# Quantile aggregation over graph neighbours: a dense layer replaced by gathered neighbour lists

## The chip, the cores and the metric

The kernel runs on one NeuronCore of one Trainium2 chip. The metric is the device time of one execution in microseconds (us). The engines are named as in the profile: PE (TensorE, matrix products), PEld (its weight loads), DVE (VectorE), ACT (ScalarE), POOL (GpSimd), SP (SyncE, which here only issues transfers). SBUF is the on-chip memory of 128 partitions, PSUM the accumulators that PE writes.

## The reference

For 16 graphs (batches) of 1024 nodes with 64 channels, cut to what matters:

```python
h = relu(layernorm(x))                      # x: (16, 1024, 64)
neigh = (adj > 0) & ~eye                    # symmetric, each edge with probability about 1/128
nb, rank = count and running number of the neighbours in each row
skip = where(nb > 10, (nb + 1) // 2, 1)
rem = neigh & (skip > 1) & (rank % skip == skip - 1) & mask;  rem |= rem.T
nd = (adj with 1 on the diagonal, without rem) > 0     # kept neighbours and the node itself
s = sort(where(nd, h[neighbour], inf))      # per node and channel, over the neighbours
nv = nd.sum()
agg = sum over (tau, w) of ((0.25, 0.25), (0.5, 0.5), (0.75, 0.25)):
        w * linear interpolation of s at tau * (nv - 1)
y = (relu((h + agg) @ W1 + b1) @ W2 + b2) * mask       # 64 -> 128 -> 64
return x + y
```

In the inputs of this case (counted from the reference's own data) a node has about 7.5 kept neighbours beside itself and at most 22.

## The kernel before

The kernel takes any adjacency and makes no list of neighbours. Work is cut into pairs of batches and into batches.

`prep_pair` (DVE mostly): layer norm of two batches, a transpose, and a bitonic sort of 128 rows (2 batches x 64 channels) of 1024 values with the node number carried along, 55 compare-exchange stages (L181 to L191, `k`, `i`, `swap`, `move`). The sorted values go to DRAM as three bf16 terms (`sd`). A second bitonic sort (L216, L217) brings the nodes' ranks back into node order.

`prep_batch`: each 128 rows of the adjacency (512 KB, tile `at`) are loaded, compared, and scanned along the row to number the neighbours (`rk`, L254); POOL clears the diagonal with an affine select (`ne` L247, `edges` L271); dropped edges are marked (L266 to L270), and the kept adjacency is transposed on PE (L301).

`main`, per batch: 16 groups of four channels x 2 halves of the nodes x 6 order statistics (two for each of three quantiles) = 192 units. Per group, `weights` builds bucket indicators on DVE (`eq` L362, `wt` L360) and three word weights on POOL (`wt` L365). Per group and half, `pack` multiplies them with the kept adjacency (L374, 32 products) and ACT moves the result from PSUM to SBUF (L378, `packed`). Each unit runs through a chain of small products and elementwise steps on 128 x 512 tiles: `choose` (`oh` L390, `hot` L392), `words` (`sel` L397, `wd` L401, `bits` L404), `locate` (`place` L411/L413, `cand` L416, `hit` L418 on DVE, `hitw` L420 on POOL, `val` L422 on DVE) and `add` (`agg` L426). The units are software-pipelined by hand, one stage of four units in each turn of the loop, and each turn also takes one step of a background generator: the preparation of the next batch or pair. Then come the MLP and the residual.

Each engine works through its own queue in order and waits on semaphores. A scheduler in the build puts the instructions of each engine into an order of its own; an instruction without inputs that wait can move far ahead of where it is written.

Of the kernel before, what the change touches and what calls it, by code (L numbers as in the profile page):

```python
# [24 lines left out]
F32 = mybir.dt.float32  # L25
# [4 lines left out]
I32 = mybir.dt.int32  # L30
U8 = mybir.dt.uint8
# [8 lines left out]
NT = N // P  # L40
NG = 16
NB = 32
HALF = 512
NSEL = 6
WEIGHTS = (0.25, 0.5, 0.25)
EPS = 1e-5
FIELDS = ((0, 11), (11, 11), (22, 10))


@with_exitstack  # L50
def quantile_graph_layer(
# [24 lines left out]
    kb = cst.tile([P, cbf.shape[1]], BF16, name="kb")  # L76
    nc.sync.dma_start(out=kb, in_=cbf)
    kf = cst.tile([P, cf32.shape[1]], F32, name="kf")
    nc.sync.dma_start(out=kf, in_=cf32)
# [37 lines left out]
    xs, hT, rankT, sorted_d = {}, {}, {}, {}  # L117
    nd, bucket, word_w, maskc = {}, {}, {}, {}

# [421 lines left out]
```

## Time and profile before

| what | value |
|---|---|
| median of 3 runs | 18762.58 us (18743.5 to 18764.14) |
| the profiled execution: span, first to last instruction | 18769.8 us |
| its own time beside the span | the page gives none; the span is 7.2 us over the median of the runs |
| PE busy | 15007.5 us, 80% of the span, 55296 products |
| DVE busy | 15816.9 us, 84%, 19847 instructions |
| POOL busy | 7256.0 us, 39%, 4293 instructions |
| ACT busy | 3137.9 us, 17% |
| DMA | 98.46 MB, mean 5 GB/s |

How to read the rows that follow: a group row reads "line, engine, operation, output <- inputs, shape of output <- shape of input, count | busy us of the group, mean ns of one instruction | idle time of its engine just before them and what ended most of it". A timeline row reads "start us, duration us, engine, line, operation". Durations of neighbouring DVE instructions overlap a little in the records, so the distance from start to start tells what one costs in a row of many. The issue of a transfer is not counted as busy time of the engine that issues it.

### The profile page before, as it was taken

What the parts mean: (1) busy time and instruction counts of PE and PEld (TensorE: products, weight loads), DVE (VectorE), ACT (ScalarE), POOL (GpSimd) and SP (SyncE); (2) the same over time, 40 slices, a digit from 0 to 9 for tenths busy, and PEclk for the clock granted to TensorE, in tenths of its full rate; (3) what the DMA queues carried; (4) which work ended last, traced back from release to release, by engine and by line L of the source; (5) the groups of instructions that cost most, each with busy time, mean ns of one, the idle gap of its engine ahead of it and who ended that gap; (6) DMA issues with size and microseconds to landing.
All of it is one profiled execution on the core that took longest, in us unless ns stands there. A gap on an engine that the chain in (4) does not pass through costs nothing. (4 is left out here: it accounts for less than half of the span.)

```text
span 18769.8 us, 153006 instructions
## 1 busy us (share of the span) xinstructions
PE 15007.5 (80%) x55296; PEld 5255.5 (28%) x55296; DVE 15816.9 (84%) x19847; ACT 3137.9 (17%) x5402; POOL 7256.0 (39%) x4293
## 2 busy tenths in 40 slices
PE   2887788777888788887788887888878887788888
PEld 0222222222222222222222222222222222223333
DVE  9898878988789887898878988789887898877777
ACT  0111111111111111111111111111111111111111
POOL 1333443334433344333443334433343333443333
PEclk6999999999999999999999999999999999999999
DMA  0000000000000000000000000000000000000000
GB/s 23 4 1 3 10 8 4 1 3 12 8 2 1 3 12 8 2 1 3 12 8 2 1 3 12 8 2 1 3 12 9 1 2 2 12 6 1 2 1 1
DMA packets 183963, 98.46 MB, mean 5 GB/s; under 512 B 163426, under 2 KB 163618, under 8 KB 183202
## 3 DMA queue, kind: packets, MB, share of 16 engines
q1 hardware_dynamic: 183202, 88.68, 1.8%
q8 instruction: 433, 7.09, 0.2%
q14 instruction: 328, 2.69, 0.0%
HBM read 78.14 MB, written 10.49 MB: 5 GB/s over the span
## 5 line engine op out<-in xcount | busy, mean ns | idle before, releaser
L420 POOL TENSOR_TENSOR hitw<-hit,coef 128x512 bf16<-128x512 bf16 x3072 | 5080.3, 1654 | 9836.9 <-DVE hit L418 9596.5
L426 PE MATMUL agg<-val,kf 128*64 128x512 f32 x6144 | 3445.6, 643 | 2079.5 <-DVE val L422 2071.6
L374 PE MATMUL pk<-kept,wt 128*128 128x512 fp8e4 x16384 | 4170.5, 385 | 278.2 <-POOL wt L365 155.5
L397 DVE TENSOR_TENSOR sel<-packed,hot 128x2048 f16<-128x2048 f16 x3072 | 4090.9, 1335 | 123.3 <-ACT hot L392 115.6
L422 DVE TENSOR_TENSOR val<-cand,hitw 128x512 f32<-128x512 f32 x3072 | 2113.5, 688 | 1976.9 <-POOL hitw L420 1884.2
L401 PE MATMUL wd<-sel,kb 128*128 128x512 f16 x9216 | 2650.1, 391 | 744.4 <-DVE sel L397 742.6
L392 ACT CAST hot<-oh 128x512 f16<-128x512 f32 x3072 | 1797.1, 585 | 7573.1 <-PE oh L390 3841.7
L416 PE MATMUL cand<-hot,table 128*128 128x512 f16 x9216 | 2674.7, 396 | 0.0
L404 DVE TENSOR_SCALAR bits<-wd,ki 128x512 int32<-128x512 int32 x3072 | 2278.7, 742 | 124.4 <-PE wd L401 122.2
L378 ACT ACTIVATE packed<-pk 128x512 f16<-128x512 f32 x2048 | 1223.2, 597 | 6859.8 <-PE pk L374 6858.1
L418 DVE TENSOR_TENSOR hit<-place,want 128x512 bf16<-128x512 f32 x3072 | 2099.5, 683 | 319.2 <-PE place L413 308.0
L374 PEld LDWEIGHTS <-wt 128*128 128x128 fp8e5 x16384 | 1593.4, 99 | 2507.5 <-POOL wt L365 380.5
L365 POOL TENSOR_TENSOR wt<-eq,ww 128x1024 fp8e5<-128x1024 bf16 x768 | 1824.9, 2400 | 724.0 <-DVE eq L362 473.2
L426 PEld LDWEIGHTS agg<-val,kf 128*64 128x64 f32 x6144 | 599.5, 137 | 3576.8 <-DVE val L422 3447.8
L401 PEld LDWEIGHTS <-kb 128*128 128x128 bf16 x9216 | 921.1, 100 | 2088.2 <-issue 1155.6
L413 PE MATMUL place<-bits,kb 128*128 128x512 bf16 x3072 | 1253.2, 408 | 97.9 <-DVE bits L404 96.8
L390 PE MATMUL oh<-below,kb 128*128 128x512 f16 x3072 | 1197.6, 390 | 163.8 <-ACT hot L392 137.9
L383 DVE TENSOR_TENSOR below<-packed,want 128x1536 f16<-128x1536 f16 x1024 | 1254.7, 1225 | 3.9 <-ACT want L337 3.4
L416 PEld LDWEIGHTS <-table 128*128 128x128 bf16 x9216 | 869.5, 100 | 1325.0 <-issue 629.9
L411 PE MATMUL place<-sel,kb 128*128 128x512 f16 x3072 | 1215.8, 396 | 14.6 <-DVE hit L418 14.4
L399 PE MATMUL wd<-hot,kb 128*128 128x512 f16 x3072 | 1200.9, 391 | 0.0
L413 PEld LDWEIGHTS <-kb 128*128 128x128 bf16 x3072 | 304.1, 99 | 1512.5 <-issue 1402.5
(97 smaller groups left out, 7443.2 us busy)
## 6 DMA issues: line engine op xcount, KB each, us to landing
at<-in_adj_dram SPq DMA_DIRECT2D x128, 512.0 KB, 3.6
table<-sd SPq DMA_DIRECT2D x768, 8.0 KB, 1.7
sd<-term SPq DMA_DIRECT2D x24, 256.0 KB, 2.0
xt<-in_x_dram SPq DMA_DIRECT2D x16, 256.0 KB, 4.0
out_dram<-res SPq DMA_DIRECT2D x16, 256.0 KB, 2.6
kb<-in_cbf_dram SPq DMA_DIRECT2D x1, 320.0 KB, 2.7
mu<-in_nodemask_dram SPq DMA_DIRECT2D x16, 1.0 KB, 4.7
kf<-in_cf_dram SPq DMA_DIRECT2D x1, 126.0 KB, 2.6
```

The lines of the kernel that those rows point to most:

```text
L365: nc.gpsimd.tensor_tensor(dst(n + 1), eq, wb, OP.mult, saturate=False)
L374: nc.tensor.matmul(pk, wt[:, t, n, :], kept[:, t, half * HALF:(half + 1) * HALF], start=(t == 0), stop=(t == NT - 1),)
L392: nc.scalar.copy(hot, oh)
L397: nc.vector.tensor_tensor(sel, packed, hot[:, None, :].to_broadcast([P, 4, HALF]), OP.mult)
L401: nc.tensor.matmul(wd, fields[n], sel[:, n + 1], start=False, stop=(n == 2))
L404: nc.vector.tensor_scalar(bits, wd.bitcast(I32), shift, 0x40000000, OP.logical_shift_left, OP.bitwise_and)
L413: nc.tensor.matmul(at, prefix, hi, start=False, stop=True)
L416: nc.tensor.matmul(cand, table[g // 4][:, n, g % 4, :], hot, start=(n == 0), stop=(n == 2))
L418: nc.vector.tensor_tensor(hit, at, want[:, half, s], OP.is_equal)
L420: nc.gpsimd.tensor_tensor(hitw, hit, coef[:, half, s], OP.mult)
L422: nc.vector.tensor_tensor(val, cand, hitw, OP.mult)
L426: nc.tensor.matmul(agg[half], pick[:, 60 - 4 * g:124 - 4 * g], val, start=False, stop=(g == NG - 1 and s == NSEL - 1),)
```

## The change

The dense method stays in the file as `dense_layer`, as a loop over pairs of batches with nothing woven beside it, and runs only if a flag is set. In its place `list_layer` computes all 16 batches:

- `load`, `drop`, `keep`: the same kept adjacency, made on PE and ACT: sign of the adjacency, its transpose, running counts as products with a triangular matrix (`rk`), the dropped edges `rem` (DVE), and the kept edges (`kp`, relu on ACT). `code`: a product that packs each row's kept neighbours as 256 words of four bits.
- `order`: nodes are ordered by their number of kept neighbours, so that the first tile of 128 nodes has the longest lists; `perm` is the permutation as a 0/1 matrix. `rem` and `perm` take turns in one buffer (tag `wide`, bufs=1).
- `collect`: the permuted words (PE), then the largest eight of them at a time with `max` and `match_replace` on DVE, which give the lists in order of neighbour number (`idx`).
- `fetch`: one indirect DMA on POOL's queue per list position and tile of 128 nodes: 128 rows of 64 floats from the table of `h` in DRAM into slot `s` of a tile `g`. By tile the lists hold 13, 11, 11, 10, 9, 8, 7, 6 rows (`CAPS`): 75 gathers for a batch. The 32 nodes with the longest lists of eight batches go through 2 x 24 gathers more (`fetch_group`, tile `gg`).
- `sort`: a sorting network over the slots, each compare-exchange a `min` (L881) and a `max` (L882) on DVE with two SBUF inputs over 128 x (128, 384, 256, 256) floats for a pair of batches (L887 where one end is enough); then each sorted slot times its interpolation weight (L892) and a product with the identity that adds it up in PSUM. `let_go` writes a one-element memset to a tile `pause` (L868) after each 0.8 us of such work as estimated in the code; nothing reads `pause`.
- `finish`: 8 gathers for a batch bring the MLP's rows back into node order; mask, residual, store.
- the main loop fetches pair m, sorts pair m - 1, and weaves the preparation of batches 2m + 2 and 2m + 3 between.
- at the end a flag is 1 if any node had more kept neighbours than its list holds; each engine loads it and branches.

The diff, cut to its core:

```diff
+CAP = 24
+TOP = 19
+CAPS = (13, 11, 11, 10, 9, 8, 7, 6)
+CLASSES = (((0,), 13), ((1, 2, 3), 11), ((4, 5), 9), ((6, 7), 7))
+FEW = 32
+GROUP = 8
...
 @with_exitstack
-def quantile_graph_layer(
+def dense_layer(
...
-    drain(prep_pair(0))
-    drain(prep_batch(0))
-    for pr in range(B // 2):
...
+    with tc.For_i(0, B, 2) as first:
+        first_b.append(first)
+        drain(prep_pair(0))
+        for b in range(2):
+            drain(prep_batch(b))
+            main(b, iter(()))
...
+    def load(b):
...
+            at = wk.tile([P, N], F32, name="at", bufs=2)
+            nc.sync.dma_start(out=at, in_=adj[b, t * P:(t + 1) * P, :])
+            sg = wk.tile([P, N], BF16, name="sg")
+            nc.scalar.activation(sg, at, AF.Sign)
+            for n in range(2):
+                tp = psum.tile([P, 4, P], F32, name="tp", tag="mx", bufs=4)
...
+                nc.scalar.activation(
+                    ne[:, 4 * n:4 * n + 4, t * P:(t + 1) * P], tp, AF.Relu, saturate=False
+                )
...
+    def drop(b):
...
+        rem = wk.tile([P, NT, N], BF16, name="rem", tag="wide", bufs=1)
...
+                nc.scalar.activation(dist[:, n * HALF:(n + 1) * HALF], rk, AF.Abs, bias=bias[:, t:t + 1])
+            nc.vector.tensor_scalar(rem[:, t], dist, half[:, t:t + 1], None, OP.is_equal)
...
+    def keep(b):
...
+                kp = psum.tile([P, 4, P], F32, name="kp", tag="mx", bufs=4)
+                nc.tensor.matmul(kp, plus, ne[:, 4 * n:4 * n + 4, ts], start=True, stop=False)
+                nc.tensor.matmul(kp, minus, rem[:, 4 * n:4 * n + 4, ts], start=False, stop=False)
+                for s in range(4):
+                    at = (4 * n + s) * P
+                    nc.tensor.matmul(kp[:, s], rem[:, t, at:at + P], minus, start=False, stop=(s == 3))
+                nc.scalar.activation(kept[:, 4 * n:4 * n + 4], kp, AF.Relu, saturate=False)
...
+                nc.tensor.matmul(
+                    code[:, s], kept[:, s], nibble, start=(s == 0), stop=(s == NT - 1), skip_group_check=True
+                )
+            nc.scalar.copy(pack[:, t, :KEYS], code.rearrange("p s k -> p (s k)"))
...
+        perm = wk.tile([P, NT, N], BF16, name="perm", tag="wide", bufs=1)
+        for t in range(NT):
+            nc.vector.tensor_scalar(perm[:, t], iota, place_f[:, t:t + 1], None, OP.is_equal)
...
+    def collect(b):
...
+            flat = psum.tile([P, KEYS + 1], F32, name="codeP", tag="code", bufs=2)
+            code = flat[:, :KEYS].rearrange("p (s k) -> p s k", k=33)
+            nc.tensor.matmul(flat, ones16[0:1], base, start=True, stop=False)
+            for t in range(NT):
+                nc.tensor.matmul(flat, perm[:, t, k * P:(k + 1) * P], pack[:, t], start=False, stop=(t == NT - 1))
...
+            for at in range(lo, hi, 8):
+                nc.vector.max(keys[:, at:at + 8], left)
+                if at + 8 < hi:
+                    nc.vector.match_replace(rest, keys[:, at:at + 8], left, 0.0)
+                    left = rest
...
+        idx = wk.tile([P, PASSED[-1] + NT], I32, name="idx", bufs=4)
+        nc.vector.tensor_scalar(idx, found, float(N), 0.0, OP.min, OP.max)
...
+    def fetch(m, halves=(0, 1)):
...
+            for k in tiles:
+                for h in halves:
+                    idx, tab = lists[2 * m + h], tables[2 * m + h]
+                    for s in (*range(CAPS[k] - 1), slots - 1):
+                        at = PASSED[-1] + k if s == slots - 1 else PASSED[k] + s
+                        nc.gpsimd.indirect_dma_start(
+                            out=g[:, s, h, k - tiles[0]], out_offset=None, in_=tab,
+                            in_offset=bass.IndirectOffsetOnAxis(ap=idx[:, at:at + 1], axis=0),
+                        )
...
+    def let_go(held):
+        if held < 0.8:
+            return held
+        nc.vector.memset(pause, 0.0)
+        return 0.0
+    def sort(g, slots, top, coef, acc):
...
+        held = 0.0
+        for lo, hi, low, high in NETWORKS[slots]:
+            pa, pb = where[lo], where[hi]
+            if low and high:
+                nc.vector.tensor_tensor(g[:, spare], g[:, pa], g[:, pb], OP.min)
+                nc.vector.tensor_tensor(g[:, pb], g[:, pa], g[:, pb], OP.max)
+                where[lo], spare = spare, pa
+                yield 2 * cost
+            else:
+                to = pa if low else pb
+                nc.vector.tensor_tensor(g[:, to], g[:, pa], g[:, pb], OP.min if low else OP.max)
+                yield cost
+            held = let_go(held + cost * (low + high))
+        for s in range(top):
+            v = g[:, where[s]]
+            nc.vector.tensor_tensor(v, v, coef(s).to_broadcast(shape), OP.mult)
+            nc.tensor.matmul(acc, ident32, v, start=False, stop=(s == top - 1))
+            held = let_go(held + cost)
...
+    def fetch_group(grp):
...
+        for k in range(n):
+            for s in range(CAP):
+                nc.gpsimd.indirect_dma_start(
+                    out=g[:, s, k], out_offset=None, in_=tab,
+                    in_offset=bass.IndirectOffsetOnAxis(ap=idx[:, k, s:s + 1], axis=0),
+                )
...
+    def finish(b):
...
+        for t in range(NT):
+            nc.gpsimd.indirect_dma_start(
+                out=yn[:, t], out_offset=None, in_=ys[b],
+                in_offset=bass.IndirectOffsetOnAxis(ap=place_of[:, b, t:t + 1], axis=0),
+            )
...
+    def prepare(b):
+        yield from both(drop(b), load(b + 1) if b + 1 < B else iter(()), normalize(b))
+        yield from keep(b)
+        yield from order(b)
+        yield from collect(b)
...
+    drain(load(0), prepare(0))
+    fetch(0, (0,))
+    drain(prepare(1))
+    pairs, per = B // 2, GROUP // 2
+    ready, waiting = [], []
+    for m in range(pairs + 1):
+        begun = [finish(b) for b in ready[:2]]
+        ready = ready[2:]
+        for g in begun:
+            next(g)
+        work = []
+        if m < pairs:
+            if m % per == per - 1:
+                fetch_group(m // per)
+                work.append(aggregate_group(m // per))
+            fetch(m, (0, 1) if m else (1,))
+        if m:
+            work.append(aggregate(m - 1))
+            waiting += [2 * m - 2, 2 * m - 1]
+        side = chain(*(prepare(b) for b in (2 * m + 2, 2 * m + 3) if b < B))
+        weave(chain(*work, *begun, (1.0,)), 115.0 if m else 1.0, side, 85.0)
+        grouped = GROUP * ((m + 1) // per)
+        ready += [b for b in waiting if b < grouped]
+        waiting = [b for b in waiting if b >= grouped]
+    drain(*(finish(b) for b in ready))
...
+    keep = ctx.enter_context(tc.tile_pool(name="keep", bufs=1))
+    flag = keep.tile([1, 1], I32, name="flag")
+    list_layer(tc, x, adj, nodemask, W1, b1, W2, b2, cbf, cf32, out, flag)
+    full = tc.nc.values_load(flag[0:1, 0:1], min_val=0, max_val=1)
+    with tc.If(full > 0):
+        dense_layer(tc, x, adj, nodemask, W1, b1, W2, b2, cbf, cf32, ci32, out)
```

The two programs differ in all their rows, so the places that matter are shown from each apart. POOL's queue in the dense method, somewhat into the program: elementwise products for the units and affine selects for the next batch.

```order
L247 AFFINE_SELECT ne<-ne 128x128
L420 TENSOR_TENSOR hitw<-hit,coef 128x512 x5
L271 AFFINE_SELECT edges<-edges 128x128
L420 TENSOR_TENSOR hitw<-hit,coef 128x512 x3
L365 TENSOR_TENSOR wt<-eq,ww 128x8x128 x3
```

POOL's queue in `list_layer` for the last pair and the second group (tiles g_18313 to g_18440 are the four classes of pair 7, `gg` the group, `yn` the rows of `finish`):

```order
L857 DMA g_18313<-htab,idx 128x64 x13
L857 DMA g_18340<-htab,idx 128x64 x32
L857 DMA g_18313<-htab,idx 128x64 x7
L953 DMA gg<-gtab,gat 128x64 x48
L857 DMA g_18313<-htab,idx 128x64 x6
L857 DMA g_18340<-htab,idx 128x64 x32
L857 DMA g_18405<-htab,idx 128x64 x34
L857 DMA g_18440<-htab,idx 128x64 x26
L977 DMA yn<-yd,place_of 128x64 x64
```

POOL no longer computes: its queue is 1424 gathers in a row (the 150 of each pair, 96 for two groups, 128 for `finish`). The first eight of all have no wait on one another; each later one waits for the one eight places ahead to land.

DVE's queue in the dense method, in the middle of a batch: the elementwise steps of the units (`hit`, `val`, `bits`), with stages of the next pair's sort between them.

```order
L404 TENSOR_SCALAR bits<-wd,ki 128x512
L184 TENSOR_TENSOR k_6740<-k_6646 128x256x2
L187 TENSOR_TENSOR move<-i_6647 128x512
L418 TENSOR_TENSOR hit<-place,want 128x512
L189 TENSOR_TENSOR move<-move,swap 128x512
L182 TENSOR_TENSOR k_6875<-k_6740 128x512
L422 TENSOR_TENSOR val<-cand,hitw 128x512
```

DVE's queue in `list_layer` near the end, where the second group's sort (`gg`) and the first exchanges of pair 7's last tile (g_18440) stand, and then, some 120 rows on, the end of the group's sort and the sort of pair 6 (g_16106 is its first tile):

```order
L881 TENSOR_TENSOR gg<-gg 128x128
L882 TENSOR_TENSOR gg<-gg 128x128
L881 TENSOR_TENSOR g_18440<-g_18440 128x256
L881 TENSOR_TENSOR gg<-gg 128x128
L882 TENSOR_TENSOR g_18440<-g_18440 128x256
```

```order
L892 TENSOR_TENSOR gg<-gg,gcoef 128x128
L882 TENSOR_TENSOR gg<-gg 128x128
L892 TENSOR_TENSOR gg<-gg,gcoef 128x128 x2
L882 TENSOR_TENSOR g_16106<-g_16106 128x128
L881 TENSOR_TENSOR g_16106<-g_16106 128x128
```

The scheduler has put the first exchanges of pair 7 ahead of the sort of pair 6, and so behind them in DVE's queue 590 rows are left: the rest of the group, nearly all of pair 6, and all of pair 7. No memset stands between these exchanges.

DVE's queue at the start of `list_layer`, where constants and the first batch's layer norm are made:

```order
L868 MEMSET pause 128x1 x10
L551 CAST kw<-kb 128x545
L868 MEMSET pause 128x1
L589 TENSOR_SCALAR pack<-kf 128x8
L868 MEMSET pause 128x1 x19
L581 CAST mask<-mu 128x128
L868 MEMSET pause 128x1 x10
L561 CAST iota<-iota_i 128x1024
L868 MEMSET pause 128x1 x6
```

The memsets, which wait for nothing, have moved ahead: of 996, 493 stand before the first exchange of all, 229 directly between two instructions of a sort, and none among the last 1738 of the 2672 instructions of the sorts.

More of the change, by code (lines that the diff above doesn't have):

```diff
@@ L73, in quantile_graph_layer @@
     dram = ctx.enter_context(tc.tile_pool(name="dram", bufs=2, space=bass.MemoryType.DRAM))
[L76 to L79, printed above, removed]
+    kb = cst.tile([P, BF_AT], BF16, name="kb")
+    nc.sync.dma_start(out=kb, in_=cbf[:, :BF_AT])
+    kf = cst.tile([P, F32_AT], F32, name="kf")
+    nc.sync.dma_start(out=kf, in_=cf32[:, :F32_AT])
     ki = cst.tile([P, ci32.shape[1]], I32, name="ki")
@@ L419, in locate @@
             hitw = wk.tile([P, HALF], BF16, name="hitw")
-            nc.gpsimd.tensor_tensor(hitw, hit, coef[:, half, s], OP.mult)
+            nc.vector.tensor_tensor(hitw, hit, coef[:, half, s], OP.mult)
             val = wk.tile([P, HALF], F32, name="val")
@@ new lines, in ones_col, with wanted, batcher @@
+def ones_col(pool, nc):
+    t = pool.tile([P, 1], F32, name="ones_c")
+    nc.vector.memset(t, 1.0)
+    return t
+def wanted(n):
+    return -(-3 * (n - 1) // 4) + 1
+def batcher(n):
+    size = 1 << (n - 1).bit_length()
+    pairs, p = [], 1
+    while p < size:
+        k = p
+        while k >= 1:
+            for j in range(k % p, size - k, 2 * k):
+                for i in range(min(k, size - j - k)):
+                    if (i + j) // (2 * p) == (i + j + k) // (2 * p) and i + j + k < n:
+                        pairs.append((i + j, i + j + k))
+            k //= 2
+        p *= 2
+    return pairs
```

454 lines of the change are left out of this document (437 added, 17 removed), and 4 rows, old and new, of the table SHORT.

## The prediction

> **What bounds the kernel now.** I read the page's engine rows first, then its groups, then the waits, then stretches of the timeline.
>
> ```profile
> PE 15007.5 (80%) x55296; PEld 5255.5 (28%) x55296; DVE 15816.9 (84%) x19847; ACT 3137.9 (17%) x5402; POOL 7256.0 (39%) x4293
> L420 POOL TENSOR_TENSOR hitw<-hit,coef 128x512 bf16<-128x512 bf16 x3072 | 5080.3, 1654 | 9836.9 <-DVE hit L418 9596.5
> L374 PE MATMUL pk<-kept,wt 128*128 128x512 fp8e4 x16384 | 4170.5, 385 | 278.2 <-POOL wt L365 155.5
> L397 DVE TENSOR_TENSOR sel<-packed,hot 128x2048 f16<-128x2048 f16 x3072 | 4090.9, 1335 | 123.3 <-ACT hot L392 115.6
> L378 ACT ACTIVATE packed<-pk 128x512 f16<-128x512 f32 x2048 | 1223.2, 597 | 6859.8 <-PE pk L374 6858.1
> ```
>
> DVE is busy for 84% and PE for 80%: no engine is idle enough to matter, and the 3072 units of the dense method (x3072 in the rows) set the time, 18,770 / 3072 = 6.1 us a unit. So the amount of work bounds it, not one wait. The waits confirm it: the longest that holds DVE is the one for `hitw`, a tenth of the span.
>
> ```profile
> DVE val L422 <- POOL hitw L420: 1884.2, 2049, 3.6
> ```
>
> **The change part by part.** All of the units, both bitonic sorts and the bucket weights go, 15,817 us of DVE and 15,008 us of PE. So the new time is built up from nothing, not subtracted. The sum stands against the profiled execution, span 18,769.8 us, 7 us (0.04%) over the median of the runs shown; beside a change of this size that is nothing.
>
> *DVE.* In a row of many, what counts is start to start.
>
> ```profile
> 107.48 0.67 DVE L181 TENSOR_TENSOR swap<-k 128x512 f16<-128x512 f32 x1
> 108.08 0.41 DVE L187 TENSOR_TENSOR move<-i 128x512 f16<-128x512 f16 x1
> ...
> 210.97 1.22 DVE L211 SCALAR_TENSOR_TENSOR kp<-i,iota 128x1024 f32<-128x1024 f16 x1
> 212.10 1.22 DVE L270 SCALAR_TENSOR_TENSOR edges<-d,ne 128x1024 bf16<-128x1024 bf16 x1
> ...
> 20.15 0.14 DVE L257 TENSOR_SCALAR skip<-rk 128x1 int32<-128x1 f16 x1
> 20.21 0.21 DVE L259 TENSOR_SCALAR many<-rk,mk 128x1 f32<-128x1 f16 x1
> ...
> 21.85 0.48 DVE L266 TENSOR_SCALAR d<-rk,first 128x1024 bf16<-128x1024 f16 x1
> 22.25 0.69 DVE L143 TENSOR_SCALAR h<-h 128x1024 f32<-128x1024 f32 x1
> ```
>
> A fp32 step with two inputs costs 0.60 us for 512 elements and 1.13 for 1024: 0.07 us and 1.04 ns an element. So 128, 256 and 384 elements cost 0.20, 0.34 and 0.47 us. A pair's sorts are 97 instructions of 128, 77 of 384 and 92 of 256 elements: 19 + 36 + 31 = 86 us, and 689 for eight pairs. Two groups: 544 of 128, 109 us. The 996 memsets at the 0.06 to 0.07 us of the [P, 1] steps: 65 us, half of it at the start, where DVE waits for loads anyway. A batch's preparation: `rem` and `perm` 16 x 0.40, 13 maxima and 5 replacements of 256 at 0.34 to 0.42, the rest some 60 small ones: 25 to 28 us, some 420 in all. DVE in sum about 1,270 us.
>
> *PE.* The transposes and fp8 products show two speeds, and the granted clock in the stretches says when (columns: stretch, length, then busy us of PE, PEld, DVE, ACT, POOL; clock; DMA share; GB/s):
>
> ```profile
> 331.58 0.61 PE L301 MATMUL et<-kb,edges 128*128 128x128 bf16 x8 [0.86 <-DVE kept L302]
> 336.58 1.01 PE L301 MATMUL et<-kb,edges 128*128 128x128 bf16 x8 [0.72 <-DVE kept L302]
> 9004.21 1.89 PE L374 MATMUL pk<-kept,wt 128*128 128x512 fp8e4 x8
> 9002.76 1.07 PE L426 MATMUL agg<-val,kf 128*64 128x512 f32 x2 [0.93 <-DVE val L422]
> 100.00:200.00 100.00, 0.00 (x0) 0.00 (x0) 100.00 (x218) 0.00 (x0) 0.00 (x0) 0.50 0.00 0
> 9000.00:9400.00 400.00, 316.82 (x1212) 112.51 (x1212) 340.47 (x400) 67.10 (x116) 178.23 (x104) 0.95 0.05 14
> ```
>
> A product of up to 128 columns costs 0.08 us (0.13 at the lower clock), one of 512 0.24, one of fp32 1.07 for two instructions. A batch has 328 of the first kind, 64 wide ones and 72 of 265 columns: 26 + 14 + 10 with small rest, 59 us, 90 at the low clock; a pair's fp32 products 33. PE in sum 1,200 us, 1,700 at worst: beside DVE, not over it.
>
> *A batch's lists as a chain.* `rem` and `perm` share one buffer, so two batches' lists can't overlap much, and from step to step ACT, PE and DVE wait for one another. From ACT's 0.60 us per 128 x 512 eviction: `drop` with the next `load` 32 evictions and 8 signs of 1,024 elements, 27 us; `keep` 16 and 8 shorter ones, 20 with its products; `order` 8; `perm` 3; `collect` 18 + 7. That is 84, with hand-overs 94 us (an estimate). Four batches stand at the start, where nothing else covers them: 4 x 94 and a first load of 24, **400 us**. Later ones lie beside the gathers.
>
> *The gathers.* No indirect DMA is in this trace. The nearest plain transfer of 128 short pieces, and small POOL instructions while DVE works without pause:
>
> ```profile
> L315 SPq DMA_DIRECT2D table<-sd x768: 302/430/1575, 206.9 to 17709.3; - x192
> table<-sd SPq DMA_DIRECT2D x768, 8.0 KB, 1.7
> L271 POOL TENSOR_SCALAR_AFFINE_SELECT edges<-edges 128x128 bf16<-128x128 bf16 x10 | 11.9, 1187 | 250.0 <-DVE edges L270 249.9
> L247 POOL TENSOR_SCALAR_AFFINE_SELECT ne<-ne 128x128 bf16<-128x128 bf16 x11 | 11.8, 1070 | 30.8 <-DVE ne L246 30.8
> 13.02 0.29 POOL L247 TENSOR_SCALAR_AFFINE_SELECT ne<-ne 128x128 bf16<-128x128 bf16 x1 [11.14 <-DVE ne L246]
> 14.40 2.21 POOL L247 TENSOR_SCALAR_AFFINE_SELECT ne<-ne 128x128 bf16<-128x128 bf16 x1 [1.09 <-DVE ne L246]
> 14.24 4.70 DVE L254 TENSOR_TENSOR_SCAN rk<-ne 128x1024 f16<-128x1024 bf16 x2
> 435.78 2.00 POOL L420 TENSOR_TENSOR hitw<-hit,coef 128x512 bf16<-128x512 bf16 x1 [5.18 <-DVE hit L418]
> ```
>
> Lower bound: SP's issue, 0.43 us. Upper: 2.0 us, what a POOL instruction takes behind a DVE instruction of two inputs. I take 1.2 us, by the two affine selects of the first 420 us, since they too are short POOL instructions amid a full DVE. Landing in 1.7 us does not limit them, with eight in flight. Fetches of pairs 1 to 7 (1050), both groups (96) and the `finish` gathers among them (64) make 1210 gathers: 1210 x 1.2 = **1,452 us**. That is over DVE's and the lists' share of the same time (12 batches x 94 = 1,130), so POOL sets these steps. For each of the seven, the first gathers wait for a list's tail: 7 x 15 = **100 us**, an estimate.
>
> *The end.* Behind the last gathered tile DVE has 590 rows left, by the prices above **183 us**; MLP of pair 7 **20** (its fp32 products at 1.07 us, eight evictions); then 48 of the last 64 `finish` gathers x 1.2 = 58, two steps of 0.60, store and branch: **83 us**.
>
> Sum: 400 + 1,452 + 100 + 183 + 20 + 83 = **2,240 us**, 0.12 of before.
>
> **The memsets.** They are to give POOL an opening between DVE's instructions. In the queue most have run ahead, and the last 1738 instructions of the sorts have none. The row at 14.40 says what that costs: POOL got through at the first boundary between two scans (14.24 + 2.29 = 16.53, end 16.61). With instructions of 0.2 to 0.47 us a boundary comes soon, so I cost their absence inside the 1.2, and their presence at nothing.
>
> **Rivals.**
>
> *Cheap gathers.* At the 0.43 us of SP's issue POOL needs 520 us for 1210 and the lists' chain sets: 400 + 1,130 + the rest of DVE 183 + 20 + 48 x 0.43 + 25 = 1,780 us. For it: SP does so in this trace. Against: SP's transfers have their addresses in the program, a gather has to read 128 of them first.
>
> *The shared port adds both up.* POOL and DVE stop one another:
>
> ```profile
> 9005.78 7.12 POOL L365 TENSOR_TENSOR wt<-eq,ww 128x1024 fp8e5<-128x1024 bf16 x3 [3.79 <-DVE eq L362]
> 9006.15 2.40 DVE L217 TENSOR_TENSOR k<-k 128x512 f32<-128x512 f32 x1
> ```
>
> L217, 0.68 us alone, took 2.40 beside POOL's products. If a gather holds DVE's sorts for its whole length, the two-input work of these steps (6 x 86 + 109, less what lies at the end, some 560 us) comes on top: 2,800 us. If each takes the blocked 2.0 us instead: 400 + 2,420 + 100 + 183 + 20 + 121 = 3,240. Against: what POOL does for a gather is to read 128 numbers and issue, so it may need the port only briefly; no row here settles it. The Trainium skill, "SBUF — State Buffer", SBUF: two separate sides, says the port pair is an exclusive lock, against two-input DVE instructions if the POOL one reads SBUF, and that descriptors of POOL's DMAs can't be written meanwhile: a transfer of about 620 ns took about 3100 ns. The trace agrees on the lock (0.29 to 2.21 us at 14.40); no run here shows it for DMAs. By its 3.1 us each the sum would be an estimated 4,630; by its 0.62 us POOL falls under the lists, and the time is near the rival before this one.
>
> *Slower than before.* If one node exceeds its list, the flag is set and `dense_layer` runs behind the lists, without anything woven in: over 18,770 + 2,240 = 21,000 us. It decides at a single node. Counted from the reference's inputs, the fullest place equals its list exactly (12 of 12 in the first tile's place 32) and none exceeds it, so it stays out unless a list goes wrong.
>
> **How the numbers follow.** About 2,240 (1,950 to 2,600): 0.52. Cheap gathers, 1,700 to 1,950: 0.18. Port or slow gathers, 2,600 to 3,300: 0.24. Dense run: 0.02. Something else, beyond 3,300: 0.04. The range from 1,750 to 3,050 leaves out some 0.05 below and 0.13 above. A measurement of this kernel tells 0.2% from no change; all cases but the dense run lie far under before, so faster 0.97, within 0.2% 0.005, slower 0.025.
>
> **What would show it.** After: 1424 gathers whose issues on POOL stand some 1.2 us apart in the middle of the span; DVE busy about 1,270 us, PE 1,200 to 1,700; no row of `dense_layer`; `pause` rows before 400 us, few after; some 185 us of sorts behind the last fetch; POOL hardly busy by the page, since it only issues. Gathers apart by over 1.6 us, or exchanges of 256 elements over 0.5 us, would mean that the port decides. Long stretches with all engines idle would mean the lists' chain.

## The result and the profile after

The changed kernel took 2368.6 us (median of four runs, 2366.6 to 2376.4) against 18763.0 us of the kernel before: a ratio of 0.1263, 95% interval 0.1261 to 0.1265. The prediction was 2,240 us, 1,750 to 3,050. On two chips tried later the very same kernel took 3,197 to 3,208 us in all of six runs (median of the five on the first of them 3,204 us, 0.1707 of before, 0.1704 to 0.1709), while the kernel before took its 18,760 us there too. On which chip the first four runs were made is not recorded. Below, "the result" is the first of the two numbers.

From the page of the changed kernel: span, engines, POOL's busy share in 40 slices, granted clock, and the three costliest groups.

```profile
span 2374.2 us, 28703 instructions
PE 1172.3 (49%) x9544; PEld 771.4 (32%) x9544; DVE 1358.8 (57%) x5409; ACT 686.8 (29%) x1328; POOL 1464.9 (62%) x1429
...
POOL 0077777777776777536477777777787777240202
PEclk9995795698869767686656968796787555555555
...
L857 POOL DMA_INDIRECT g<-htab,idx x1200 | 1237.5, 1031 | 525.9 <-issue 354.3
L881 DVE TENSOR_TENSOR g<-g 128x128 f32<-128x128 f32 (+2 forms) x904 | 363.6, 408 | 620.7 <-DMA g<-htab,idx 587.8
L893 PE MATMUL acc<-g,kf 128*128 128x256 f32 (+2 forms) x512 | 189.8, 516 | 431.9 <-DVE g L892 431.7
```

No row of `dense_layer` is left, so the second method did not run. POOL is busy in seven tenths of nearly every slice from 115 us to 2,030 us, and what DVE waits for is the gathers (587.8 us). A single gather in the timeline of POOL, and what POOL waited for:

```profile
1200.54 0.94 POOL L857 DMA_INDIRECT g<-htab,idx  x1 [0.30 <-issue]
1201.79 0.95 POOL L857 DMA_INDIRECT g<-htab,idx  x1 [0.30 <-issue]
```

```profile
DVE g L881 <- DMA g<-htab,idx: 587.8, 36, 71.1
...
POOL g L857 <- issue: 354.3, 1162, 0.3
...
POOL g L857 <- DVE idx L776: 113.0, 1, 113.0
```

A gather takes 0.95 us on POOL and 0.30 us pass before the next: 1.25 us from start to start. POOL waited once for a list, the first (113 us); after that 1162 of 1200 gathers waited for nothing but that 0.30. So the gathers on POOL set the time from 115 to 2,030 us. (This is read from the trace; no run on a chip that behaves like this one left gathers out.) This stretch of 1,915 us holds 1,360 gathers: 1,360 x 1.25 = 1,700; four holes of 12, 53, 5 and 29 us (the second ahead of the first `finish`, the others until a buffer of `g` was free) are 99; the rest, 116 us, are gathers that took longer than 0.95. What the second hole waited for, the trace does not show.

### The profile page after: what moved, and what is told of

It reads as the page before. It is cut to its first block, busy times and chain, and to the rows that moved or that the text cites. A ratio compares the mean times of both kernels' runs of the same rounds, so it can differ in the third digit from the quotient of the medians.

```text
span 2374.2 us, 28703 instructions
## 1 busy us (share of the span) xinstructions
PE 1172.3 (49%) x9544; PEld 771.4 (32%) x9544; DVE 1358.8 (57%) x5409; ACT 686.8 (29%) x1328; POOL 1464.9 (62%) x1429
## 5 line engine op out<-in xcount | busy, mean ns | idle before, releaser
L857 POOL DMA_INDIRECT g<-htab,idx x1200 | 1237.5, 1031 | 525.9 <-issue 354.3
L881 DVE TENSOR_TENSOR g<-g 128x128 f32<-128x128 f32 (+2 forms) x904 | 363.6, 408 | 620.7 <-DMA g<-htab,idx 587.8
L893 PE MATMUL acc<-g,kf 128*128 128x256 f32 (+2 forms) x512 | 189.8, 516 | 431.9 <-DVE g L892 431.7
L882 DVE TENSOR_TENSOR g<-g 128x128 f32<-128x128 f32 (+2 forms) x904 | 363.6, 408 | 48.4 <-PE acc L873 38.3
L659 PE MATMUL rk<-kw,ne 128*128 128x512 fp8e5 (+3 forms) x1280 | 311.1, 339 | 2.1 <-ACT dist L663 1.8
L663 ACT ACTIVATE dist<-rk,bias 128x512 f16<-128x512 f32 x256 | 174.0, 702 | 313.5 <-PE rk L653 144.1
L653 PE MATMUL rk<-kw,ne 128*128 128x128 fp8e5 x1024 | 198.8, 230 | 16.5 <-ACT dist L663 12.7
L680 ACT ACTIVATE kept<-kp 128x512 fp8e4<-128x512 f32 x256 | 147.5, 611 | 179.4 <-PE kp L679 178.5
L744 PE MATMUL codeP<-pack,perm 128*128 128x265 f16 x1024 | 160.3, 288 | 69.4 <-DVE perm L730 69.4
L612 ACT ACTIVATE ne<-tp 128x512 fp8e4<-128x512 f32 x256 | 142.3, 614 | 112.9 <-PE tp L611 59.7
L659 PEld LDWEIGHTS <-ne 128*128 128x128 fp8e4 x1280 | 128.6, 104 | 92.5 <-issue 40.8
L881 DVE TENSOR_TENSOR gg<-gg 128x128 f32<-128x128 f32 x248 | 71.5, 288 | 115.2 <-DMA gg<-gtab,gat 111.6
L653 PEld LDWEIGHTS <-ne 128*128 128x128 fp8e4 x1024 | 106.1, 104 | 19.3 <-issue 5.1
```

What stands on the lines that cost most here:

```text
L612: nc.scalar.activation(ne[:, 4 * n:4 * n + 4, t * P:(t + 1) * P], tp, AF.Relu, saturate=False)
L653: nc.tensor.matmul(rk[:, lo * P:(lo + 1) * P], ne[:, s, ts], upper, start=(s == 0), stop=(s == last), skip_group_check=True,)
L659: nc.tensor.matmul(rk[:, lo * P:], ne[:, s, ts], full[:, None, :].to_broadcast([P, 4 - lo, P]), start=(s == 0 and n == 1), stop=False, ski ...
L663: nc.scalar.activation(dist[:, n * HALF:(n + 1) * HALF], rk, AF.Abs, bias=bias[:, t:t + 1])
L680: nc.scalar.activation(kept[:, 4 * n:4 * n + 4], kp, AF.Relu, saturate=False)
L744: nc.tensor.matmul(flat, perm[:, t, k * P:(k + 1) * P], pack[:, t], start=False, stop=(t == NT - 1))
```

## The experiments

### The memsets: left out, and made to stay

The theory after the result: the gathers on POOL set the time, and the memsets, which mostly run ahead, do nothing. Rival: they are the openings through which POOL gets in.

```diff
     def let_go(held):
         if held < 0.8:
             return held
-        nc.vector.memset(pause, 0.0)
         return 0.0
```

> All 996 memsets of `pause` left out, nothing else changed. Theory (the gathers on POOL, 1.25 us apart, set the time from 115 to 2030 us, and most memsets stand where no gather waits): 2,345 to 2,390 us, within 1% of the 2,369 with them; gathers that take over 1.0 us on POOL stay near 362 of 1424. Rival (the memsets are the openings through which POOL gets in): gathers of over 1.0 us become more than 600, their extra time over 0.947 us rises from 115 to over 250 us, and the time to over 2,480.

```diff
-        nc.vector.memset(pause, 0.0)
+        nc.vector.memset(free[:, 0, 0, 0:1] if len(free.shape) == 4 else free[:, 0, 0:1], 0.0)
```

Here `free` is the slot of `g` that the next exchange writes (`g[:, spare]`).

> Each memset writes one element of the free slot of `g` instead of `pause`, so that in the exchanges it must stay between the max before and the next min. Theory: gathers lose 115 us in all to DVE (time over 0.947 us each), so true openings can bring back at most that, less some 20 us of memsets behind the last gather: 2,270 to 2,370. Rival (DVE's two-input work does not hold the gathers at all, their long ones have another cause): extra time of the gathers stays near 115 us, time 2,370 to 2,420.

Measured: 3193.1 us without the memsets (ratio 0.1704, 0.1700 to 0.1707) and 3269.2 with memsets that stay (0.1743, 0.1741 to 0.1745). The groups of the gathers on both pages, first without memsets, then with those that stay:

```profile
L857 POOL DMA_INDIRECT g<-htab,idx x1200 | 1186.3, 989 | 1240.5 <-issue 641.4
```

```profile
L857 POOL DMA_INDIRECT g<-htab,idx x1200 | 1155.5, 963 | 1289.8 <-issue 538.0
```

Neither theory had 3,193. The rival cannot be it: the mean gather became shorter without memsets (989 ns against 1,031), not longer. What grew is POOL's idle time ahead of these gathers, from 526 to 1,241 us. The control below, with its memsets, takes as long and has gathers of 983 ns: the memsets had no part in it. The two kernels of this section ran on one chip and can be compared: memsets that truly stand between the exchanges go with shorter gathers (963 against 989 ns, 31 us for 1200), and cost 76 us more in all.

### Half the gathers

```diff
-                    for s in (*range(CAPS[k] - 1), slots - 1):
+                    for s in (*range(0, CAPS[k] - 1, 2), slots - 1):
...
+            for s in range(1, slots - 1, 2):
+                nc.vector.memset(g[:, s], 0.0)
```

> Of the gathers of the lists (L857) only the even positions and the last slot are made, 688 instead of 1200; DVE fills the other slots with zeros by memsets, so the values are not the reference's. Theory: POOL sets the time as long as it has more work than the lists' chain, so 512 x 1.25 = 640 us go until that chain shows: 1,730 to 1,900 us, POOL no longer busy without holes. Rival (DVE's sorts or the lists set as much as POOL): above 2,100.

Measured: 2562.1 us (0.1367, 0.1363 to 0.1371). By itself this looked like the rival. Against the control of the next section but one (3,204 us, on another chip) it is 642 us less, and 512 x 1.25 = 640: each gather that is left out gives back its whole price, as though nothing ran beside it.

### Gathers without a graph

A kernel of eight stages with nothing but 120 gathers in each and some work on DVE.

> No graph work: eight stages, one after another, of 120 gathers of 128 rows of 256 B from `x` in eight buffers; zeros are stored as output. Stages: DVE idle; beside a chain of dependent min and max of 128x256 fp32; the same with a one-element memset after each max that stays there; beside two interleaved chains of 384 and 128; beside a chain of one-input steps; the two chains without gathers; 64 rows, DVE idle; rows of 64 B, DVE idle. Theory: 1.25 us apart alone, and beside DVE up to 1.4 (the mean of the busy stretches of the trace, 1.35); 64 rows about half if POOL writes row by row, 1.25 if the price is per instruction; rows of 64 B the same 1.25. Rival (a lock by DVE's two-input instructions): beside the unbroken chain 3 us or more or none until it ends, and 1.25 again with the memsets and beside one-input steps.

Measured on POOL, start to start (median): 1.252 us with DVE idle; 1.400 beside the unbroken chain of min and max, 1.252 with memsets that stay, 1.340 beside two interleaved chains, 1.252 beside one-input steps; 1.207 for 64 rows; 1.254 for rows of 64 B. So the price is per gather, not per row or byte, and DVE's two-input work, at the slow pace that it had beside them, adds 0.09 to 0.15 us. What no theory had is this slow pace of DVE. The stage of the unbroken chain:

```profile
200.09 0.42 DVE L121 TENSOR_TENSOR d_chain<-d_chain 128x256 f32<-128x256 f32 x1 [0.97 <-DVE d_chain L122]
200.25 1.09 POOL L105 DMA_INDIRECT g_chain<-in_x_dram,idx_chain  x1 [0.30 <-issue]
201.49 0.42 DVE L122 TENSOR_TENSOR d_chain<-d_chain 128x256 f32<-128x256 f32 x1 [0.97 <-DVE d_chain L121]
201.64 1.10 POOL L105 DMA_INDIRECT g_chain<-in_x_dram,idx_chain  x1 [0.30 <-issue]
```

Each step takes its usual 0.42 us, but the next starts 1.40 us later; this lasts until 15 us behind the last gather, and then they follow at 0.46. The one-input steps were held too (the first 96 stood 0.33 us apart, those after them 1.40, and those well behind the gathers 0.33 again), so it is not the two-input steps alone.

### The control, and two changes of the sorts

> The changed kernel itself once more, as a control for the four runs before it. These brought a surprise: without the memsets 3,193 us, and in that trace PE and ACT, which take no part in the sorts, wait 671 and 406 us for nothing that is shown, most of it while POOL gathers. Theory A (the memsets, or the order of the program that they bring, are worth it): 2,369 us again, within 1%. Rival B (another chip or memory placement runs everything beside gathers slower): near 3,200 us.

Measured: 3204.3 us (0.1707, 0.1704 to 0.1709), five runs within 0.4%. Rival B: the program is the same to the byte, PE, ACT and POOL execute the same instructions in the same order, and it takes 3,204 us instead of 2,369. The windows show where. Stretch 115 to 209 us, in which POOL makes the 75 gathers of the first batch in both; columns: stretch, length, busy us (and instructions) of PE, PEld, DVE, ACT, POOL, clock, DMA share, GB/s. First the result, then the control:

```profile
115.00:209.00 94.00, 58.37 (x650) 40.07 (x647) 47.86 (x290) 52.00 (x103) 71.43 (x75) 0.83 0.54 136
```

```profile
115.00:209.00 94.00, 16.50 (x121) 9.17 (x119) 6.57 (x47) 10.11 (x15) 71.30 (x75) 0.55 0.24 51
```

The same 75 gathers; beside them PE did 650 products in one and 121 in the other, ACT 103 instructions against 15. The next list is done at 168 us in the result and at 266 in the control, so POOL then waits for it. PE's timeline at the same products (L619, counts of one column), again the result first:

```profile
123.26 0.34 PE L619 MATMUL nb<-kw,ne 128*128 128x1 fp8e5 x8
```

```profile
130.87 0.21 PE L619 MATMUL nb<-kw,ne 128*128 128x1 fp8e5 x2 [0.54 <-issue]
131.59 0.10 PEld L619 LDWEIGHTS <-ne 128*128 128x128 fp8e4 x1 [0.59 <-issue]
131.60 0.18 PE L619 MATMUL nb<-kw,ne 128*128 128x1 fp8e5 x1 [0.52 <-issue]
131.80 0.94 POOL L857 DMA_INDIRECT g<-htab,idx  x1 [0.30 <-issue]
132.30 0.10 PEld L619 LDWEIGHTS <-ne 128*128 128x128 fp8e4 x1 [0.60 <-issue]
...
133.69 0.20 PE L619 MATMUL nb<-kw,ne 128*128 128x1 fp8e5 x2 [1.91 <-issue]
```

Eight products in 0.34 us there; here one every 0.7 to 2.1 us, and between them PE waits for "issue", which is nothing that the profile shows. "Starved" below means this: beside gathers an engine starts its next instruction only 0.70 us or a multiple of it after the last, though it waits for nothing that the profile shows.

Two changes of the sorts ran on the same chip as the control. In the first a copy of one element of the pair before's last product (`hold`) makes each pair's sort wait for that product, since in the trace of the result DVE stood in front of exchanges of pair 7 whose rows had not landed while pair 6's were ready.

```diff
...
+            hold(g[:, slots, 0, 0, 0:1])
             acc = psum.tile([P, 2, n, C], F32, name="acc", tag="agg")
```

> A one-element copy from the last product of pair m - 1 into the free slot of each tile of pair m, so that no exchange of pair m can stand in DVE's queue ahead of the sort of pair m - 1; the memsets of `pause` stay. Theory: behind the last gather DVE then has only pair 7 and parts of the group left, 130 to 200 us less: 2,150 to 2,280 us. Rival (what was late in the tail was late for another reason, or the order of the whole program tips as without the memsets): 2,350 us or more, at worst 3,200.

Measured: 3197.9 us (0.1706, 0.1703 to 0.1709): no change against the control. Nor did the tail become shorter: 677 of the sorts' instructions started after the last gather of a sort, 660 in the control, and 384 us followed that gather, 381 in the control. So where engines starve, another order of the pairs in DVE's queue brings nothing. On a chip that behaves like that of the result it was not run, so whether it is worth something there is open.

The second leaves the exchanges out, and with them the memsets that stand in their loop (880 of 996):

```diff
-        for lo, hi, low, high in NETWORKS[slots]:
-            ...
         for s in range(top):
```

> All compare-exchanges of the sorts left out (products with the weights stay, pads are zeros), so the values are not the reference's; the memsets stay. Theory (POOL and the lists set the time, DVE's exchanges only lengthen gathers and the end): 115 us of longer gathers and some 200 of the tail go, 2,000 to 2,100 us. Rival (gathers and exchanges exclude one another, as in the stage of 128x256 min and max beside gathers, 1.40 us for a pair of them where each alone takes 1.25 and 0.48): 1,400 to 1,800.

Measured: 2915.8 us (0.1555, 0.1553 to 0.1557). DVE's busy time fell from 1,362 to 558 us, 804 less; the time fell by 288. So over a third of DVE's saved time came off the whole, and the rest lay beside other waits; neither number of the expectation fits, and both were made from the trace of the result.

### Which engines starve, and when

> The changed kernel a third time. It took 2,369 us in the four executions behind the prediction and 3,204 in five later ones; instructions and their order on PE, ACT and POOL are the same in both traces. Theory (something outside the program sets whether the other engines run freely beside a gather): either 2,360 to 2,380 or 3,190 to 3,210 us, nothing between. Rival (a drift, or one chip that is slow): another value.

Measured: 3203.8 us, on yet another chip: the second of the two values.

> No graph work: six stages of 120 gathers of 128 rows of 256 B from `x`: beside DVE's min and max chain of 128x256; beside one-element-free memsets of 128x256; beside products of 128x128 bf16 on PE; beside copies of 128x256 on ACT; beside all three; and the three with a single gather. Theory (beside a gather every engine gets an instruction only some 0.7 us apart, as DVE did in the stages of the run before: 0.74 us a step where 0.34 to 0.48 is what it takes alone): PE's products and ACT's copies, too, stand 0.7 us or more apart beside gathers and under 0.5 alone. Rival (only the port that DVE and POOL share): PE and ACT run at their own speed, only DVE's two-input steps are held. If the third run of the changed kernel takes 2,369 us, all run at their own speed in this one.

The stage of ACT's copies (gathers from 662 to 812 us), on the same chip:

```profile
663.03 27.00 ACT L141 COPY d_act<-d_act 128x256 f32<-128x256 f32 x62 [661.00 <-DVE z L112]
690.21 0.40 ACT L141 COPY d_act<-d_act 128x256 f32<-128x256 f32 x1 [0.19 <-ACT d_act L141]
691.61 0.40 ACT L141 COPY d_act<-d_act 128x256 f32<-128x256 f32 x1 [0.99 <-ACT d_act L141]
...
828.84 0.40 ACT L141 COPY d_act<-d_act 128x256 f32<-128x256 f32 x1 [0.29 <-ACT d_act L141]
829.54 5.73 ACT L141 COPY d_act<-d_act 128x256 f32<-128x256 f32 x13 [0.30 <-ACT d_act L141]
```

62 copies at their own pace, 0.44 us, then one every 1.40 us until 17 us after the last gather, then 0.44 again. The stages of PE's products, and of DVE's memsets, which read nothing:

```profile
465.44 7.64 PE L135 MATMUL acc<-w 128*128 128x128 bf16 x83 [465.44 <-DVE w L132]
...
521.14 0.26 PE L135 MATMUL acc<-w 128*128 128x128 bf16 x1 [2.54 <-issue]
523.94 0.26 PE L135 MATMUL acc<-w 128*128 128x128 bf16 x1 [2.54 <-issue]
```

```profile
352.23 0.27 DVE L128 MEMSET d_clear<- 128x256 f32 x1 [1.13 <-DVE d_clear L128]
353.63 0.27 DVE L128 MEMSET d_clear<- 128x256 f32 x1 [1.13 <-issue]
```

Products and weight loads alternate at 1.40 us (a product every 2.80), memsets at 1.40. In the stage with all three, ACT and PE were held at this pace side by side. So in these stages a starved engine gets its next instruction 1.40 us after the last, whatever it does: the theory holds, at twice the 0.7 us that it named. The rival (only the port that DVE and POOL share) falls as the cause of 3,204 us, since PE and ACT are held in stages in which DVE has nothing to do. How much an engine executes before it starves differs: DVE's chain of min and max in this run's first stage kept its 0.46 us for 186 steps, 85 us long, the chain of the stage shown above, on another chip, for only 14.

### Which work of POOL starves them

> No graph work: copies of 128x256 on ACT, which alone are 0.44 us apart, beside five kinds of POOL work: 120 plain transfers from POOL's queue; 60 copies of 2048 elements on POOL; and 120 gathers in which POOL first waits for the landing of the last one and copies one element, after each 8; after each 24; after each 24 with a copy of 2048 elements on POOL as well. In the run before ACT made about 60 copies at its own pace and then one every 1.4 us until the gathers ended. Theory (during a gather no instructions reach the other engines beyond some 60 that wait in each, and a rest of POOL lets in new ones): with a rest after each 24 gathers (30 us) ACT keeps 0.44 us for 60 of the steps after each rest, so the 450 copies end within 230 us; after each 8 all are at 0.44. Copies on POOL do not hold ACT at all; plain transfers hold it as gathers do if the writing of descriptors is the cause. Rival (a rest of 3 us is too short, or the 60 are used up only once): ACT's copies stay near 1.0 us in the mean.

Windows of the five stages, on a fourth chip (columns: stretch, length, DVE, ACT, POOL, clock, DMA share, GB/s): plain transfers; copies on POOL; gathers with a rest after each 8; gathers with a rest after each 24, and what follows them; the whole fifth stage, gathers with a longer rest after each 24.

```profile
12.00:143.00 131.00, 2.43 (x2) 121.00 (x300) 53.66 (x102) 1.00 0.18 45
147.00:278.00 131.00, 0.20 (x2) 121.26 (x300) 112.49 (x60) 1.00 0.00 0
280.00:477.00 197.00, 0.70 (x5) 181.89 (x450) 116.40 (x134) 1.00 0.10 20
478.00:640.00 162.00, 0.85 (x2) 67.89 (x168) 114.78 (x124) 1.00 0.12 24
640.00:767.00 127.00, 0.00 (x0) 113.84 (x282) 0.00 (x0) 1.00 0.00 0
768.00:1010.00 242.00, 1.88 (x5) 181.88 (x450) 122.57 (x128) 1.00 0.08 16
```

131 us for 300 copies is 0.44 each: neither plain transfers from POOL's queue nor copies on POOL hold ACT. With a rest after each 8 gathers 450 copies took 197 us, all at 0.44. After each 24 only 168 copies fit into 162 us, and all 450 took 288. A rest is small:

```profile
406.56 0.18 POOL L119 COPY g_every<-g_every 128x1 f32<-128x1 f32 x1 [1.48 <-DMA g_every<-in_x_dram,idx_every]
406.89 0.97 POOL L121 DMA_INDIRECT g_every<-in_x_dram,idx_every  x1 [0.15 <-issue]
```

1.48 us of waiting for the landing and 0.18 us of copy. The half of the theory on rests after 8 is shown. That such a rest after 24 gives 60 more instructions is wrong: behind the first 24 gathers ACT made some ten copies at its pace, behind the later ones none. The fifth stage has the longer rest, a copy of 2048 elements on POOL behind the landing, and there the theory nearly holds. The first rest and ACT's copies behind it and behind the second:

```profile
800.47 1.89 POOL L116 COPY big<-g_longer 128x2048 f32<-128x2048 f32 x1 [1.52 <-DMA g_longer<-in_x_dram,idx_longer]
803.00 23.19 ACT L156 COPY d_longer<-d_longer 128x256 f32<-128x256 f32 x53 [0.30 <-ACT d_longer L156]
836.99 20.02 ACT L156 COPY d_longer<-d_longer 128x256 f32<-128x256 f32 x46 [0.99 <-ACT d_longer L156]
```

From the end of the 24th gather to the start of the next 3.8 us pass, against 1.8 with the short rest, and behind the four rests ACT made 53, 46, 35 and 27 copies at its pace; the 450 took 240 us. That fits an engine that lives, beside gathers, on a store of instructions which POOL's rests fill up, more in a longer one; the store itself is not shown. Why 1.8 us are enough after each 8 gathers and bring next to nothing after 24, and why the four rests bring less and less, stays open.

### Rests in the kernel

```diff
+        if before[0] is not None and count[0] % 3 == 0:
+            nc.gpsimd.tensor_copy(to[:, 0:1], before[0][:, 0:1])
         nc.gpsimd.indirect_dma_start(
```

> The changed kernel with a rest of POOL after each third gather within a fetch, a group or a `finish`: POOL copies one element of the last gathered slot into the next one, so it waits for the landing, some 1.5 us more than without. Values stay the reference's. Theory (beside gathers an engine lives on some 60 instructions that wait in it, and a rest fills them up again): some 475 rests x 1.5 = 700 us more on POOL, 1,780 + 700 + 115 before the first gather + 250 behind the last = 2,700 to 2,950 us, 3,204 without rests; PE's and ACT's waits for nothing shown, 693 and 374 us, fall to under a third. Rival (the rests cost more than they bring, since the time is the sum of gathers and everything else): 3,204 + 300 to 700.

In the other, `% 2` and `eps` in the place of `before[0][:, 0:1]`.

> The same with another rest: after each second gather POOL copies one element of a constant, which waits for nothing, 0.3 to 0.5 us more. Theory, if so short a rest already fills the waiting instructions up: 712 x 0.4 = 285 us more on POOL, 2,450 to 2,700 us. Rival (what fills them needs the 1.5 us of a landing): no starved step less, 3,204 + 285 = 3,400 to 3,500.

Measured: 2423.3 us (0.1292, 0.1289 to 0.1294) and 2435.5 us (0.1297, 0.1295 to 0.1300). That is 770 to 780 us under the control, but it is not the proof that it seems. In the second kernel the first 75 gathers have no copy between them (those copies wait for nothing and were scheduled ahead), and yet, in the window of the table above:

```profile
115.00:209.00 94.00, 55.67 (x630) 38.35 (x628) 46.44 (x293) 51.84 (x101) 71.55 (x74) 0.83 0.55 137
```

PE made 630 products beside them, as in the result (650), where starved it made 121. So this chip, the fifth of these experiments, does not starve without rests either, and what the two runs show is only what rests cost there: 55 and 67 us over the result, if the kernel without rests takes 2,369 us on this chip, where it was not run. Both times lie below what was expected of them, and neither theory nor rival is tested, since nothing starved; whether rests bring the 3,204 us of the other chips down was not tried.

## Why the prediction was right, point by point, and where not

**What sets the time**: right on the chip of the result, as its trace shows. The forecast said that POOL's gathers, 1.2 us apart, outlast DVE and the lists; they stand 1.25 us apart, and DVE is busy for 1,359 us (1,270 were predicted, from parts that add up to 1,283), PE for 1,172 (1,200 to 1,700).

**400 + 1,452 + 100 us up to the last gather of a sort**: 1,952 predicted, 2,030 measured, but by luck, with two errors that cancel. The four lists of the start were done at 115, 168, 294 and 349 us, near the 400; but I had nothing beside them, and the gathers began with the first list, at 115. On the other side 1,360 gathers lie in this stretch and not 1,210 (the 150 of the first pair, which the forecast put into the start at no price), they are 1.25 us apart and not 1.20, and holes and longer gathers came to 215 us where 100 were estimated for hand-overs.

**The shared port**, a rival at 2,800 or 3,240 us: gathers do take longer beside a busy DVE, but little. From the starts of the gathers in the result's trace, the holes left out, 566 beside an idle DVE are 1.25 us apart and 668 beside a DVE busy for over three quarters of the time 1.41 in the mean (1.35 without the 18 that are over 2.5 us apart); the longest gather took 7.93 us (its row is below). The Trainium skill, "SBUF — State Buffer", SBUF: two separate sides, has 3100 ns for a transfer of 620 ns beside DVE; the mean here is far from that, and only 8 of the 1424 gathers take 3.1 us or more.

```profile
L857 POOL DMA_INDIRECT g<-htab,idx x1200: 941/947/7930, 114.9 to 2029.9; - x172
...
L868 DVE MEMSET pause<- x996: 59/59/59, 1.1 to 1072.2; 128x1 f32 x200
```

**The end**: 183 + 20 + 83 = 286 predicted, 344 measured (window below: 602 instructions of DVE, 216 us busy). The rows left were counted well, 583 of 590; their price was not. Two rows of one sort, each waiting for the last, then three of two sorts that alternate, then two of one sort again:

```profile
1908.33 0.29 DVE L881 TENSOR_TENSOR gg<-gg 128x128 f32<-128x128 f32 x1
1908.65 0.29 DVE L882 TENSOR_TENSOR gg<-gg 128x128 f32<-128x128 f32 x1
...
1953.03 0.28 DVE L881 TENSOR_TENSOR gg<-gg 128x128 f32<-128x128 f32 x1
1953.23 0.55 DVE L881 TENSOR_TENSOR g<-g 128x384 f32<-128x384 f32 x1
1953.70 0.28 DVE L882 TENSOR_TENSOR gg<-gg 128x128 f32<-128x128 f32 x1
...
2128.06 0.56 DVE L881 TENSOR_TENSOR g<-g 128x384 f32<-128x384 f32 x1
2128.65 0.56 DVE L882 TENSOR_TENSOR g<-g 128x384 f32<-128x384 f32 x1
```

Alternating, 128 and 384 elements cost 0.20 and 0.47 us from start to start, as I had taken from rows of the kernel before, in which the next step worked on another tile. In one chain they cost 0.32 and 0.59. With one pair left nothing alternates. Beside that, PE's sums of weighted slots stood on the path, up to 6.6 us each. The granted clock is down to 0.56 there, and a product of 384 columns follows the last after 0.64 us, where it is 0.32 at a clock of 0.8 and above:

```profile
2030.00:2374.00 344.00, 113.63 (x299) 67.38 (x299) 216.32 (x602) 14.70 (x29) 62.66 (x65) 0.56 0.10 21
```

The sorts thus ended at 2,324 us, 294 after the last gather; the MLP took 26 us, and `finish` was cheaper than feared (24 us behind the MLP, not 83), because 48 of its 64 gathers fitted beside the sorts and 8 beside the MLP.

**The memsets at nothing**: right by the runs, on the chips that starve. With them 0.1707 (0.1704 to 0.1709), without 0.1704 (0.1700 to 0.1707), on two chips; made to stay, 2.3% slower than without, on one. On a chip that behaves like that of the result their absence was not run. That few stand after 400 us was wrong: 342 of the 996 do, until 1,072 us.

**POOL hardly busy by the page**: wrong, and with it the sentence that the issue of a transfer is not counted as busy time. A gather counts as 0.95 us of work of POOL, and a plain transfer from POOL's queue as 0.55.

**What no step had**: 3,204 us on other chips lies beyond the range that I gave (3,050), so that the first runs did not fall on such a chip was luck. A rival of the prediction comes near that time, a gather of 2.0 us each, but for a reason that the runs refute: the gathers stay at 1.25 us, and it is the other engines that wait, PE and ACT too, also where DVE has nothing to do. A gather then costs the kernel about its full 1.25 us, as though nothing ran beside it: 512 fewer gave 642 us back.

## What to carry to other kernels

Price a gather by its number, not by its bytes: 1.25 us of POOL for up to 128 rows, and lay the lists' chain and the sorts beside it. Before a kernel is tuned for overlap with such gathers, look in a window beside a long run of them whether the other engines keep their pace, and look on more than one chip; a rest of 1.8 us for the landing after each 8 kept ACT at its pace, while after 24 in a row it took a rest of 3.8 us to bring some 50 more instructions. Two-input steps in one chain cost 0.12 us more each than two chains that alternate; keep a second chain for the end of the work.

## What the runs showed of the hardware that was not expected

On four chips (the whole kernel ran on two of them, the one without memsets on a third, only stages on the fourth) engines beside a run of gathers execute some instructions at their pace, 62 copies on ACT, 83 products with their loads on PE, 14 to 186 steps on DVE, and then one every 1.40 us until 6 to 19 us after the last gather. In the runs of the result, and with the two kernels with rests, this is absent. Plain transfers from POOL's queue (0.55 us each on POOL) and POOL's own copies do not cause it, and a rest of 3.8 us on POOL after 24 gathers ends it for 27 to 53 copies. The Trainium skill, "Runtime: NRT & Kernel Launch", Instruction fetch mechanics, says that each engine streams its instructions in blocks over a DMA queue of its own and that this is mostly hidden; that this fetch is what is late here would fit the waits for "issue", but no run shows it, and blocks were also loaded in the middle of a starved stretch (one at 749.5 us, in 0.31 us, in the stage of ACT's copies). What makes one chip do this and another not is open, and even that it is the chip is not shown: each chip was used only once, for one group of runs, so something that is set when the program is loaded there would look the same.
